# Two pairs of score banks and four banks for the rest, a third unit of 16-wide heads in flight, and first products by sevens in three more layers

## The chip, the cores and the metric

The kernel runs on one core of a Trainium2 chip. The metric is the device time of one execution in microseconds. The core's engines work side by side, each through a queue of its own in the order in which the program was built: PE (TensorE, the matmuls, with its weight loads shown as PEld), DVE (VectorE), ACT (ScalarE), POOL (GpSimd), and SP, which here only issues transfers. Matmuls write to eight accumulator banks (PSUM) of 128 x 512 numbers in 32 bits. A bank is free for a new product when DVE or ACT has read the old one.

## What is computed

A decoder of two layers on an input of 16 sequences of 128 tokens with 256 features, all in 32 bits. Each sublayer is added to the stream and normalized. In order:

```python
x = ln(x + attn0(x))      # 16 heads of 64, causal softmax
x = ln(x + ensemble0(x))  # sum over 8 members: gate_e * proj_out_e . relu(proj_in_e . x), 256 -> 512 -> 256
x = ln(x + experts0(x))   # two shared experts, and 2 of 16 routed experts per token
x = ln(x + attn1(x))      # 16 heads of 16, softmax over a band of +-8 tokens
x = ln(x + cross1(x))     # 16 heads of 16, over a context of 128 tokens
x = ln(x + dense1(x))     # norm_g * sum over 8 experts: w2_e . gelu(w1_e . x + b1_e) + b2_e, 256 -> 512 -> 256
```

## The kernel before

The 16 sequences are four groups (`g` = 0 to 3) of four, 512 tokens each. A sublayer of a group is written as a generator. A planner, `Weaver`, draws from two of them at a time: a main stream of attention and a dense stream (ensembles and experts), by given shares of estimated time, with short follow-ups (norms, transposes, gates, routing) put in ahead of both. A line `yield UNTIL, t` gives a step a due time in the planner's clock. The dense stream's order is ensemble 0, ensemble 1, routed experts for groups 0 and 1, ensemble 2, ensemble 3, routed experts for groups 2 and 3, then the four dense layers of the second decoder layer, 0 to 3. What the planner writes down, the language's scheduler then orders once more for each engine; it gives each tile a buffer from its pool, and the instruction that first writes a reused buffer waits for its last reader.

Products of two sides are cut by a scheme that needs seven block products where eight would do it plainly (`products`): the second product of each ensemble or dense expert always goes so. The stationary blocks (`wb`) are summed once and kept in memory, the sums of the moving blocks (`cm`, L812 to L815) are made by DVE, and the seven partial results are accumulated by DVE (`acc`, L834 and L836). The first product of an expert (256 -> 512, with the hidden result `h`) goes plainly, with eight matmuls of 512 columns per expert, or by sevens with the class `Firsts`, fourteen of 256 columns. Expert 0 of a layer is plain in both cases. By sevens:

- `rows_sums` (DVE, L720) forms sums of the activations once for a layer, in two buffers of the tag `hT`.
- `weight_sums` (POOL, L720 and L746) forms sums of the weights of each expert, in two of the four buffers of the tag `cw`. Routing (`plan`), the gates of the ensembles (`gates0`, `chose`) and the collection of results also use `cw`.
- `steps` runs the seven products in a bank `sums`, held over all four steps, and further banks `other`. ACT copies `sums` to `h` three times (L777, L782, L786) and DVE adds `other` three times (L771). Then `done` applies the relu and the gate (DVE) or Gelu (ACT).

Attention goes by units. In `attention0` a unit is four heads of 64 of one sequence, in `attention16` eight heads of 16 (half the heads of one sequence). A unit passes through score products (`psS`), softmax (`e`: DVE, ACT, and the final scaling on POOL, L380), transposes of the weights (`psO` from `e`, copied by ACT to `eT`, L390), the product with the values, and the output product. In `attention16` POOL first makes masked keys (`kb`, L515). A loop runs over units with fixed distances between these steps, written as `m = n - 2` and the like; `e` has three buffers (tag `p` of the pool `p3`).

The eight banks are shared as follows: score tiles (tag `S`) take two banks each, one such tile in the program; everything else (`bank`, tag `B`: names psH, psM, psO) has six banks.

Of the kernel before, what the change touches and what calls it, by code (L numbers as in the profile page):

```python
# [8 lines left out]
F32 = mybir.dt.float32  # L9
# [5 lines left out]
P = 128  # L15
# [16 lines left out]
def kernel(ctx: ExitStack, tc: tile.TileContext, a: dict, out: bass.AP):  # L32
# [14 lines left out]


    def bank(tag):
        return ps.tile([P, T], F32, tag="B", name=f"ps{tag}", bufs=6)  # L50

    recent = [None]

# [342 lines left out]
    def attention0(x, g):  # L396
        norm = Norm(x)
        norm.bias(bo0)

        def project_quad(g, j):  # L400
            wq, wk, wv, wo = first_quads[j] if g == 0 and j < 2 else load_quad(j)
            xT = xTs[g]
            qT = p2.tile([P, 2, T], F32, tag="qT", name="qT")
            kT = p2.tile([P, 2, T], F32, tag="kT", name="kT")
            for i in range(2):
                c = 2 * j + i
                cols = slice(i * P, (i + 1) * P)
                pq = bank("H")
                project(pq, wq, cols, xT)
                nc.vector.tensor_scalar(  # L410
                    qT[:, i, :], pq, bq0[:, c:c + 1], 0.125, ALU.add, ALU.mult
                )
                pk = bank("H")
                project(pk, wk, cols, xT)
                nc.scalar.activation(kT[:, i, :], pk, AF.Identity, bias=bk0[:, c:c + 1])
                yield 3.44

            v = yield from values(xT, wv, KC)
            heads0[g, j] = qT, kT, v, wo

        def scores(j, b):
            qT, kT, _, _ = heads0[g, j]
            at = slice(b * P, (b + 1) * P)
            s = ps.tile([P, 2, T], F32, tag="S", name="psS", bufs=1)[:, :, :D].rearrange(
                "p s (i k) -> p s i k", i=2
            )

            for i in range(2):
                for k in range(2):
                    rows = slice(64 * k, 64 * k + 64)  # L430
                    with joined(i == k == 0):
                        mm(
                            s[:, k, i, :], lhsT=qT[rows, i, at], rhs=kT[rows, i, at],
                            start=True, stop=True,
                        )
            return softmax(s, causal)

        def output(j, b, zT):
            po = bank("H")[:, :D]
            for i in range(2):  # L440
                mm(po, lhsT=zT[:, i, :], rhs=heads0[g, j][3][:, i, :], start=i == 0, stop=i == 1)
            norm.add(b, po, last=j == 3)

        if (g, 0) not in heads0:
            yield from project_quad(g, 0)
        units = [(j, b) for j in range(4) for b in range(GB)]
        e, eT, zT, at = {}, {}, {}, {}
        for n in range(len(units) + 5):
            if n < 16:
                j, b = units[n]  # L450
                e[n] = scores(j, b)
                at["e", n] = weaver.now + 9.0
                yield 0.6
            m = n - 2
            if m in e:
                yield UNTIL, at["e", m]
                eT[m], _ = weights_T(e.pop(m))
                at["t", m] = weaver.now + 2.5
                yield 0.5
            m = n - 5  # L460
            if m in zT:
                yield UNTIL, at["z", m]
                output(*units[m], zT.pop(m))
                yield 0.86
            m = n - 4
            if m in eT:
                j, b = units[m]
                yield UNTIL, at["t", m]

                pz = bank("O")[:, :D].rearrange("p (c q) -> p c q", c=2)  # L470
                got = eT.pop(m)
                for i in range(2):
                    for k in range(2):
                        h = 2 * i + k
                        with joined(h == 0):
                            mm(
                                pz[64 * k:64 * k + 64, i, :],
                                lhsT=heads0[g, j][2][:, b, 64 * h:64 * h + 64],
                                rhs=got[:, 2 * k + i, :], start=True, stop=True,
                            )  # L480
                zT[m] = p3.tile([P, 2, P], F32, tag="z", name="zT")

                nc.vector.tensor_tensor(  # L483
                    zT[m], pz, bv0[:, 2 * j:2 * j + 2].unsqueeze(2).to_broadcast([P, 2, P]), ALU.add
                )
                at["z", m] = weaver.now + 2.5
                yield 0.6
            if n < 16 and (n < 12 or g + 1 < NG):

                j, b = units[n]  # L490
                if b == 0:
                    ahead = project_quad(g, j + 1) if j < 3 else project_quad(g + 1, 0)
                yield next(ahead)
                if b == 3:
                    assert next(ahead, None) is None
        assert not e and not eT and not zT
        norm.done()


    def attention16(x, qT, kT, v, bv, wo, bo, seen):  # L500
# [9 lines left out]
        def scores(b, c):  # L510

            at = slice(b * P, (b + 1) * P)

            kb = p2.tile([P, 4, P], F32, tag="kb", name="kb")
            nc.gpsimd.tensor_tensor(  # L515
                kb, kT[:, c, at].unsqueeze(1).to_broadcast([P, 4, P]),
                hm4.unsqueeze(2).to_broadcast([P, 4, P]), ALU.mult,
            )
            yield UNTIL, weaver.now + 2.0
            s = ps.tile([P, 2, T], F32, tag="S", name="psS", bufs=1)  # L520
            s = s[:, :, :4 * keys].rearrange("p s (h k) -> p s h k", h=4)
            for k in range(2):
                rows = slice(64 * k, 64 * k + 64)
                for queries, key, _ in parts:
                    mine = slice(b * P + queries.start, b * P + queries.stop)
                    with joined(k == 0 and key == 0):
                        mm(
                            s[queries, k], lhsT=qT[rows, c, mine],
                            rhs=kb[rows, :, key:key + keys], start=True, stop=True,
                        )  # L530
            return softmax(s, seen)
# [37 lines left out]

        units = [(b, c) for b in range(GB) for c in range(2)]  # L570
        e, eT, zT, at = {}, {}, {}, {}
        for n in range(len(units) + 5):
            if n < 8:
                e[n] = yield from scores(*units[n])
                at["e", n] = weaver.now + 12.0
                yield 1.06
            m = n - 2
            if m in e:
                yield UNTIL, at["e", m]
                got = e.pop(m)  # L580
                eT[m] = [weights_T(got[:, 4 * k:4 * k + 4, :]) for k in range(2)]
                at["t", m] = weaver.now + 3.5
                yield 1.0
            m = n - 4
            if ("z", m) in at and units[m][1] == 1:
                yield UNTIL, at["z", m]
                output(units[m][0])
                yield 0.86
            m = n - 3
            if m in eT:  # L590
                yield UNTIL, at["t", m]
                weigh(*units[m], eT.pop(m))
                at["z", m] = weaver.now + 3.0
                yield 0.63
# [337 lines left out]
    def ensemble0(x, xT, g):  # L932
# [13 lines left out]
        def done(to, got, e, i, j):  # L946
# [10 lines left out]
            lambda t: after(  # L957
                products_end(t, norm, None, lambda norm, b: norm.done(b, 2)), tail(1, g)
            ),
            Firsts(xT, done) if g in () else None,  # L960
        )

    def small(tag, n=16, bufs=None):
# [391 lines left out]
    def experts1(x, xT, g, ng):  # L1355
        def load(e):
            return load_up(f"we1_{e}", a["L1_ffn_w1"][e])[0]

        def hidden(h, up, e, c):
            ph = bank("H")  # L1360
            project(ph, up, slice(c * P, (c + 1) * P), xT)
            gelu(h, ph, e, c)

        def gelu(to, one, e, c):
            nc.scalar.activation(to, one, AF.Gelu, bias=b1[:, 4 * e + c:4 * e + c + 1])  # L1365

        def done(to, got, e, i, j):
            for q in range(2):
                gelu(to[:, q], got[:, q], e, 2 * i + q)

        norm = Norm(x)
        for b in range(GB):
            nc.vector.scalar_tensor_tensor(
                out=x[:, b, :], in0=b2sum, scalar=ng[:, b:b + 1], in1=x[:, b, :],
                op0=ALU.mult, op1=ALU.add,
            )
        yield from products(
            load, lambda e: load_blocks(1, e, g, a["L1_ffn_w2"][e]), hidden,
            lambda t: after(products_end(t, norm, ng, lambda norm, b: store(norm, g, b))),
            Firsts(xT, done) if g in (2,3) else None,  # L1380
        )


# [158 lines left out]
```

## Time and profile before

| what | value |
|---|---|
| median of three runs | 1738.57 us (1735.91 to 1738.95) |
| profiled execution, its own time | 1738.27 us |
| span of its trace | 1736.6 us |
| TensorE busy | 1647.3 us, 95% of the span |
| mean granted TensorE clock | 0.975 |
| DVE, ACT, POOL busy | 1164.0, 591.8, 505.5 us |
| stages by time | attention of groups 0 and 1 to about 211 us; ensembles 0 and 1 beside attention of groups 2 and 3 to 545; routing to 615; routed experts to 673; ensembles 2 and 3 beside the second decoder layer's attention to 1040; routed experts to 1144; dense layers after it, alone from 1535 |

The span runs from the first to the last instruction; the execution's own time has 1.7 us around it. Busy time of TensorE includes matmuls that overlap in its pipeline, so the gaps between matmuls, and the granted clock, say more than the share of 95%. In a list of waits a line reads: who waited, for whom, us in total, how many times, the longest. The idle time of an engine that doesn't set the end costs nothing.

### The profile page before, as it was taken

How to read it: one execution, taken by the hardware profiler on the slowest of the kernel's cores; microseconds unless marked ns; L12 is line 12 of the kernel's file. 1: busy time of each engine (PE TensorE's matmuls, PEld its weight loads, DVE VectorE, ACT ScalarE, POOL GpSimd, SP SyncE). 2: the span in 40 equal slices, each digit the busy share in tenths (PEclk: the TensorE clock that was granted, in tenths of full speed). 3: DMA queues.
4: the chain of work that ended last, by engine and by line, in shares of the span. 5: the costliest groups of instructions: out<-in, count | busy, mean ns of one | idle time of the engine just before them, and what ended most of it. 6: DMA issues, size and time to landing. Idle time of an engine off the chain costs nothing.

```text
span 1736.6 us, 22830 instructions
## 1 busy us (share of the span) xinstructions
PE 1647.3 (95%) x8196; PEld 1080.5 (62%) x8196; DVE 1164.0 (67%) x2330; ACT 591.8 (34%) x1360; POOL 505.5 (29%) x543
## 2 busy tenths in 40 slices
PE   9999999999999799999899988998999999999996
PEld 6665656666656465656556655665665665588785
DVE  4565565576677534878796875858769675965655
ACT  4434411111022242103131212643846372654342
POOL 5443532220002302312241315334224132522220
PEclk9999999999998899999999989999999999999998
DMA  9533533432330458422223204671222221124330
GB/s 272 174 118 123 172 140 111 150 112 103 103 110 13 146 186 290 153 93 82 90 79 104 80 31 170 202 245 64 68 91 80 71 70 67 63 83 134 113 121 34
DMA packets 98192, 204.52 MB, mean 118 GB/s; under 512 B 16136, under 2 KB 58176, under 8 KB 98016
## 3 DMA queue, kind: packets, MB, share of 16 engines
q1 hardware_dynamic: 92176, 179.53, 31.2%
q0 software_dynamic: 5904, 23.54, 3.7%
q8 instruction: 65, 1.06, 0.2%
q14 instruction: 47, 0.39, 0.1%
HBM read 172.43 MB, written 37.81 MB: 121 GB/s over the span
## 4 chain that ended last, share of the span: by engine, by line
PE 75%; DVE 12%; DMA 4%; issue 3%; POOL 2%; ACT 1%; SPq 1%; another core or an unknown queue 0%; POOLq 0%; DVEq 0%; ACTq 0%
PE psH L55 40%; PE psM L55 21%; PE psO L60 5%; PE psS L55 4%; PE psO L55 3%; PE psH L60 2%; DVE nmax L358 1%; DVE e L364 1%; DMA wquad<-in_L_attn_W_Q 1%; DMA rows<-copies 1%; DVE total L370 1%; DVE x L311 1%; DVE x L293 1%; DVE acc L836 1%; POOL got L1303 1%
## 5 line engine op out<-in xcount | busy, mean ns | idle before, releaser
L55 PE MATMUL psH<-xT,we 128*128 128x512 f32 (+1 forms) x856 | 397.4, 590 | 0.5 <-DMA we<-in_L_xattn_proj_in 0.5
L380 POOL TENSOR_TENSOR e<-e,inv 128x512 f32<-128x512 f32 (+2 forms) x121 | 159.4, 1319 | 425.6 <-DVE inv L378 369.7
L55 PE MATMUL psM<-cm,wb 128*128 128x256 f32 x1024 | 263.6, 381 | 0.0
L55 PEld LDWEIGHTS psH<-xT,we 128*128 128x128 f32 x856 | 156.8, 191 | 137.0 <-issue 124.9
L55 PEld LDWEIGHTS psM<-cm,wb 128*128 128x128 f32 x1024 | 192.0, 190 | 52.2 <-issue 25.7
L55 PE MATMUL psM<-h,wb 128*128 128x256 f32 x768 | 200.8, 384 | 5.0 <-ACT h L1365 3.4
L836 DVE TENSOR_TENSOR acc<-psM,acc 128x512 f32<-128x512 f32 (+1 forms) x216 | 134.5, 624 | 98.3 <-PE psM L55 98.2
L390 ACT COPY eT<-psO 128x512 f32<-128x512 f32 (+1 forms) x192 | 105.5, 584 | 275.6 <-PE psO L60 261.3
L55 PEld LDWEIGHTS psM<-h,wb 128*128 128x128 f32 x768 | 143.0, 190 | 54.8 <-issue 29.3
L373 ACT ACTIVATE e<-e,nmax 128x128 f32<-128x128 f32 x256 | 99.5, 390 | 139.6 <-DVE nmax L358 113.4
L942 DVE SCALAR_TENSOR_TENSOR h<-psH,gt 128x512 f32<-128x512 f32 x128 | 87.6, 685 | 71.5 <-PE psH L55 71.2
L55 PE MATMUL psH<-xT,wquad 128*128 128x512 f32 x256 | 117.2, 601 | 6.1 <-DMA wquad<-in_L_attn_W_Q 5.4
L515 POOL TENSOR_TENSOR kb<-kT,hm 128x512 f32<-128x512 f32 x64 | 72.4, 1134 | 159.1 <-PE psS L55 104.5
L60 PEld LDWEIGHTS psO<-ident,e 128*128 128x128 f32 (+1 forms) x768 | 85.2, 133 | 48.2 <-issue 35.9
L60 PE MATMUL psO<-ident,e 128*128 128x128 f32 (+1 forms) x768 | 109.7, 280 | 2.0 <-POOL e L380 2.0
L1365 ACT ACTIVATE h<-psH,b 128x512 f32<-128x512 f32 (+1 forms) x100 | 60.6, 623 | 104.7 <-PE psH L55 95.9
L369 ACT ACTIVATE e<-e 128x576 f32<-128x576 f32 (+1 forms) x64 | 55.7, 871 | 88.2 <-DVE e L364 87.9
L55 PEld LDWEIGHTS psH<-xT,wquad 128*128 128x128 f32 x256 | 46.7, 190 | 58.9 <-issue 47.8
L309 POOL TENSOR_TENSOR rstd<-ve,mhalf 128x4 f32<-128x4 f32 (+1 forms) x32 | 28.9, 903 | 177.9 <-DVE ve L307 177.6
L370 DVE TENSOR_REDUCE total<-e 128x8 f32<-128x576 f32 (+1 forms) x64 | 62.8, 981 | 24.6 <-ACT e L369 24.0
L55 PE MATMUL psO<-eT,v 128*64 128x128 f32 (+2 forms) x1024 | 76.6, 313 | 0.0
L55 PE MATMUL psH<-wquad,zT 128*128 128x256 f32 x256 | 67.8, 388 | 4.8 <-DVE zT L483 2.5
(240 smaller groups left out, 2624.0 us busy)
## 6 DMA issues: line engine op xcount, KB each, us to landing
wb<-wbd SPq DMA_DIRECT2D x56, 896.0 KB
we<-in_L_xattn_proj_in SPq DMA_DIRECT2D x32, 512.0 KB
wt<-table SPq DMA_DIRECT2D x64, 256.0 KB
we<-in_L_ffn_w SPq DMA_DIRECT2D x32, 512.0 KB
wbd<-wb POOLq DMA_DIRECT2D x16, 896.0 KB
gt<-gatesd SPq DMA_DIRECT2D x32, 256.0 KB
results<-y SPq DMA_DIRECT2D x10, 768.0 KB
rows<-copies SPq DMA_DIRECT2D x6, 1024.0 KB
```

The source lines that it names most:

```text
L55: recent[0] = nc.tensor.matmul(*args, **how)
L60: return nc.tensor.transpose(out_, in_, ident[:n, :n])
L309: nc.gpsimd.tensor_tensor(rstd[:, at], ve[:, at], mhalf[:, at], ALU.pow)
L369: nc.scalar.activation(e, e, AF.Exp)
L370: nc.vector.tensor_reduce(total, e, AX.X, ALU.add)
L373: nc.scalar.activation(e[:, h, :], s[:, h // (n // 2), h % (n // 2), :], AF.Exp, bias=nmax[:, h:h + 1], accum_out=total[:, h:h + 1],)
L380: engine.tensor_tensor(e, e, inv.unsqueeze(2).to_broadcast([P, n, keys]), ALU.mult)
L390: return eT, nc.scalar.copy(eT, pt)
L515: nc.gpsimd.tensor_tensor(kb, kT[:, c, at].unsqueeze(1).to_broadcast([P, 4, P]), hm4.unsqueeze(2).to_broadcast([P, 4, P]), ALU.mult,)
L836: nc.vector.tensor_tensor(to, pm[:, :len(slots), :], to, ALU.add)
L942: nc.vector.scalar_tensor_tensor(out=h, in0=ph, scalar=0.0, in1=gates[e], op0=ALU.max, op1=ALU.mult)
L1365: nc.scalar.activation(to, one, AF.Gelu, bias=b1[:, 4 * e + c:4 * e + c + 1])
```

## The change

Three edits.

1. The banks: the tag `B` goes from six banks to four, the tag `S` from one tile of two banks to two tiles. Eight banks are in use as before.
2. In `attention16` the distances of the steps grow by one: transposes of a unit come three scores later, the product with the values four, the output five.
3. `Firsts` is used for the first products of the ensembles of groups 0 and 1, and of the dense layer of group 1; before, only the dense layers of groups 2 and 3 had it.

```diff
     def bank(tag):
-        return ps.tile([P, T], F32, tag="B", name=f"ps{tag}", bufs=6)
+        return ps.tile([P, T], F32, tag="B", name=f"ps{tag}", bufs=4)
...
         def scores(j, b):
...
-            s = ps.tile([P, 2, T], F32, tag="S", name="psS", bufs=1)[:, :, :D].rearrange(
+            s = ps.tile([P, 2, T], F32, tag="S", name="psS", bufs=2)[:, :, :D].rearrange(
...
             yield UNTIL, weaver.now + 2.0
-            s = ps.tile([P, 2, T], F32, tag="S", name="psS", bufs=1)
+            s = ps.tile([P, 2, T], F32, tag="S", name="psS", bufs=2)
...
-        for n in range(len(units) + 5):
+        for n in range(len(units) + 6):
             if n < 8:
                 e[n] = yield from scores(*units[n])
                 at["e", n] = weaver.now + 12.0
                 yield 1.06
-            m = n - 2
+            m = n - 3
             if m in e:
...
-            m = n - 4
+            m = n - 5
             if ("z", m) in at and units[m][1] == 1:
...
-            m = n - 3
+            m = n - 4
             if m in eT:
...
-            Firsts(xT, done) if g in () else None,
+            Firsts(xT, done) if g in (0,1) else None,
...
-            Firsts(xT, done) if g in (2,3) else None,
+            Firsts(xT, done) if g in (1,2,3) else None,
```

## The prediction

> **What bounds the kernel now.** I read four views. First the page: busy time per engine and the clock row.
>
> ```profile
> span 1736.6 us, 22830 instructions
> ...
> PE   1647.3 (95%) x8196; PEld 1080.5 (62%) x8196; DVE 1164.0 (67%) x2330; ACT 591.8 (34%) x1360; POOL 505.5 (29%) x543
> ```
>
> TensorE is the bound as a whole: 89 us of the span are without it, no other engine is above 67%. The table by stage (columns: length, then busy us of PE, weight loads, DVE, ACT, POOL, then granted clock, DMA share, GB/s) tells where those 89 us lie.
>
> ```profile
> 50.00:100.00 50.00, 47.38 (x289) 30.96 (x288) 27.23 (x54) 22.65 (x82) 21.93 (x27) 1.00 0.41 141
> 211.00:545.00 334.00, 332.29 (x1418) 209.41 (x1418) 211.91 (x411) 54.65 (x192) 68.38 (x95) 1.00 0.33 114
> 545.00:615.00 70.00, 56.30 (x294) 37.23 (x293) 41.84 (x117) 22.50 (x86) 18.49 (x19) 0.85 0.27 91
> 615.00:673.00 58.00, 52.90 (x319) 38.41 (x317) 20.21 (x59) 26.14 (x74) 0.00 (x0) 0.94 0.72 245
> 1040.00:1144.00 104.00, 92.61 (x537) 60.90 (x536) 67.70 (x133) 47.22 (x111) 41.64 (x33) 0.95 0.57 186
> 1144.00:1535.00 391.00, 376.93 (x1877) 230.93 (x1877) 287.90 (x535) 205.46 (x280) 135.87 (x113) 0.99 0.25 85
> 1535.00:1720.00 185.00, 182.48 (x840) 156.35 (x839) 114.61 (x215) 74.97 (x155) 42.99 (x55) 1.00 0.33 107
> ```
>
> Where an ensemble or a dense layer runs (211 to 545, and from 1535), TensorE idles 1.7 us in 334 and 2.5 in 185: a product removed there is time removed. The idle time sits around routing (545 to 615) and the routed experts (615 to 673, 1040 to 1144), which the edits don't shorten. The list of waits, TensorE's own, shows what the score banks cost; the timeline shows one such gap (in brackets: idle time before, and its releaser).
>
> ```profile
> PE psS L55 <- DVE e L352: 7.7, 7, 2.2
> PE psS L55 <- DVE e L364: 3.9, 4, 1.8
> PE psO L60 <- POOL e L380: 2.0, 2, 1.1
> 57.83 0.71 PE L55 MATMUL psS<-kT,qT 64*128 64x128 f32 x8 [0.86 <-DVE e L352]
> ```
>
> Last the chain in order of time, four plain first products of 512 columns, and then one expert of a layer that already has first products by sevens (a matmul is two records, so x16 is eight):
>
> ```profile
> 930.11 3.43 PE psH L55 x8
> ...
> 1659.90 3.45 PE psM L55 x16
> 1663.36 0.86 PE psH L55 x4
> 1664.22 0.86 PE psM L55 x4
> 1665.09 0.86 PE psH L55 x4
> 1665.95 2.59 PE psM L55 x12
> 1668.54 0.86 PE psH L55 x4
> 1669.40 1.73 PE psM L55 x8
> 1671.13 0.86 PE psH L55 x4
> 1671.99 3.45 PE psM L55 x16
> ```
>
> The expert takes 12.09 us, back to back, for 28 products of 256 columns: 0.432 us each.
>
> **The change part by part.** The sum is made against the profiled execution, 1738.27 us (span 1736.6 and 1.7 around it); the median of the runs is 1738.57, so 0.3 is added at the end. It counts on the order in which the two programs issue their instructions, which the changed kernel's build gives (no time is in it).
>
> *First products by sevens, ensembles g=0 and 1, dense layer g=1.* Per expert 1 to 7, eight products of 512 columns go and fourteen of 256 come. Four of 512 take 3.43 us (the first line of the fence), so eight take 6.86; fourteen at 0.432 take 6.05. That is 0.81 us by 7 experts by 3 layers: **-17.0 us**, all on the bound engine, in stages without gaps.
> What comes with it lies beside TensorE. DVE: three additions per expert of 0.688 us (row L771) and four subtractions of 0.418 per layer: 63 x 0.688 + 12 x 0.418 = 48 us; the ensembles' four relu-and-gate steps per expert stay four of 512 elements (0.685). ACT: three copies of 0.586 per expert, 37 us; in the dense layer eight Gelu of 256 (0.50 and 0.46) for four of 512 (0.688), 8 us more; six table loads of 1.283 fewer by the built order, 8 us less. POOL: three of 0.73 and one of 0.81 per expert, 63 us. The totals become DVE 1212, ACT 629, POOL 568 of some 1720 us: 70, 37 and 33%, still cover. If DVE's cover were gone, its 48 us would be the price. No DMA is added; the weight loads keep their three buffers.
> The additions wait for ACT's copy and for TensorE. In DVE's queue they stand ahead of the accumulations and the gating, which TensorE's next banks wait for. POOL's weight sums wait for a load or for a `cw` buffer, which the gate layer also uses (its eight `chose` tiles fall into ensemble g=1); behind them in POOL's queue stand the softmax scaling (L380) and the key masks (L515). In the built order the scaling has at least 5.6 us of TensorE work as cover beyond the first 190 us of that work, as before (5.1). I take **+1 us** for all of this: the only layers with sevens in the trace lose 0.83 and 0.28 us to the copy L782 and nothing to POOL. Ends: 0 and +12 (half a microsecond at each of 21 experts, and 1.5 at the shared buffers).
>
> *Second pair of score banks, third unit.* The waits of the fence and one of 0.2 sum to 13.8 us. In the built order the waits of score matmuls for DVE fall from 89 to 31. The five 0.86 us gaps of the first layer had no TensorE work between a score and the next; now they have 0.43, so 0.43 us each is left (2.2). The rest have 1.7 or more. So at most -11.6. A gap removed from a queue in order is partly met again at the next wait, so I take half: **-6 us** (ends 0 and -11.6).
> The third unit has its limits. The tile `e` has three buffers (p3), so the softmax of unit n, which writes `e` on DVE (L352, or L364 after its maximum), must wait for the transposes of unit n-3. The built order shows four units scored and three in softmax at most steps, before three and two: the unit is real. Behind that waiting DVE step stand the accumulations of the dense layer.
>
> *Four banks for the rest.* The trace of before has no bank shortage, so I bound it. The cover of a wait is the TensorE work between the last matmul that the releaser depends on and the matmul that waits. Waits with under 1.5 us of cover go from 61 to 169: in the routed experts from 21 to 102, elsewhere from 40 to 67.
> What a release costs, by rows: DVE starts 0.03 us after TensorE ends, and a bank of 512 takes 0.69:
>
> ```profile
> 1638.16 1.03 PE L55 MATMUL psM<-tx,we 128*128 128x256 f32 x4
> 1639.22 0.69 DVE L771 TENSOR_TENSOR h<-psM,h 128x512 f32<-128x512 f32 x1 [0.17 <-PE psM L55]
> ```
>
> So 0.8 us of cover is enough if the reader's queue is empty; one step ahead of it costs up to 0.69. In the routed experts the new bank wait is for the copy L1242, 0.266 us against 0.43 of cover: free, unless the tanh (0.28), a copy (0.37) or an exponential (1.06) stands ahead on ACT. There are 34 waits under 0.7 us there (before: 1). At 0.3 us that is 10; I take 5, since the first such stage is held by its loads (DMA busy at 1.0 of its 16 engines from 640 to 660). Elsewhere 27 more, with DVE busy two thirds of the time, at a quarter of a microsecond: 7. Together **+12 us**; ends 0 and 108 x 0.35 = 38.
>
> A rule that speaks against the change: the Trainium skill, "TensorE: Matmul & The Clock Gate", section "A second HAM failure mode: psum-queue depth-cycling", says that cycling through accumulator banks leaves TensorE micro-idle so often that its clock falls back and forth. The row comes first: from 50 to 100 it idles 2.6 us in short gaps and the clock stays 1.00. With the row the 12 us cost 12. By the rule the two expert stages (58 and 104 us, at 0.94 and 0.95) could fall to the 0.85 of 545 to 615, some 16 us more, 1745. I take the row, and keep the 16 for the upper end.
>
> Sum: 1738.27 - 17.0 + 1 - 6 + 12 = 1728.3; with 0.3, **1728 us**.
>
> **The rivals.**
> 1. *Bank shortage outweighs the products (slower).* Place: the 108 new short covers, in the expert stages and where DVE is over 70% busy (287.9 of 391 us from 1144 to 1535). With a reader's step ahead at every second one, 0.35 us each: 1738.3 - 17 + 1 - 6 + 38 = 1754. It makes the kernel slower by more than the bound from 0.24 us per short cover on. For it: banks fall by a third. Against: covers of 0.43 to 0.85 left gaps of 0.2 to 0.5 us before, or none, outside the chains of norms and routing.
> 2. *A late POOL or DVE takes the gain (no change).* The weight sums hold up the softmax scaling or DVE meets its buffer waits for `e`: +11 beside the sum, 1739. For: the trace has POOL waiting up to 8 us for TensorE at L720. Against: the cover of L380 above.
> 3. *The second score pair and the third unit do nothing*, because the gaps move to the next wait: 1734.6.
> 4. *Banks cost next to nothing*, as the 40 short covers elsewhere do before, and the score waits go: 1738.3 - 17 + 1 - 11 + 3 = 1714.
>
> **How the numbers follow.** Forecast 0.42 (own range 1721 to 1735), rival 4 0.18, rival 3 0.12, rival 2 0.10, rival 1 0.18. A measurement of this kernel tells about 0.2% from no change, 3.5 us: faster is below 1735.1, slower above 1742. Rival 3 lies on that edge and is split. Faster 0.68, same 0.14, slower 0.18. The range goes from rival 4 to the middle of rival 1 (with part of the clock's 16 us): 1713 to 1748.
>
> **What would show it.** Right: TensorE's busy time down by some 17 us; the stage of the two ensembles shorter by about 11 us and still with hardly a gap; waits of psS for DVE from 11.6 us to about 2 to 5; new waits of TensorE for ACT (L1242, L1257, L390) and DVE in the expert stages, 5 to 10 us; clock there as before. Wrong: waits of psH, psM or psO for DVE or ACT of over 25 us in total (rival 1), or for POOL L720 or L380 of over 5 (rival 2); or a clock under 0.9 in the expert stages.

## The result, and the profile after

The change makes the kernel slower: 1750.64 us (median of six runs, 1744.91 to 1753.72) against 1738.80 for the kernel before (six runs, 1735.91 to 1742.33), a ratio of 1.0064 with a 95% interval of 1.0046 to 1.0082. That is some 11 us more, where I forecast 10 less. The profiled execution is the fastest of the six (1744.91 us, span 1743.2), so its trace shows 6.6 us of the difference to the profiled execution before, not the whole. Part of the rest is TensorE's granted clock: 0.979 in this execution, 0.974 to 0.977 in the other five (0.003 of 1743 us is some 5 us, an estimate).

First the page of the changed kernel, span and busy time per engine.

```profile
span 1743.2 us, 23681 instructions
...
PE 1636.8 (94%) x8448; PEld 1126.1 (65%) x8448; DVE 1209.6 (69%) x2406; ACT 626.0 (36%) x1445; POOL 577.3 (33%) x626
```

The work is as forecast: DVE 1209.6 (1212 was said), ACT 626.0 (629), POOL 577.3 (568). The columns that TensorE is given, at the 3.43 us for four products of 512, fall by 18 us. Its busy time fell by only 10.5 (1647.3 to 1636.8), not by the 17 that I had named as a sign, and the time without TensorE grew from 89 us (1736.6 - 1647.3) to 106 (1743.2 - 1636.8). The table by stage of the changed kernel (length, busy us of PE, weight loads, DVE, ACT, POOL, granted clock, DMA share, GB/s), with the stages of the prediction's table from the ensembles to the end of attention, shows where.

```profile
207.00:529.00 322.00, 321.58 (x1569) 239.96 (x1570) 240.08 (x454) 76.20 (x225) 112.67 (x147) 1.00 0.35 117
529.00:599.00 70.00, 55.29 (x306) 37.34 (x305) 43.39 (x121) 24.16 (x95) 18.56 (x19) 0.90 0.26 91
599.00:658.00 59.00, 53.47 (x317) 38.72 (x317) 19.77 (x58) 25.88 (x72) 0.00 (x0) 0.94 0.71 239
1030.00:1138.00 108.00, 96.92 (x536) 63.49 (x534) 68.03 (x137) 48.51 (x110) 41.36 (x33) 0.94 0.55 179
1138.00:1545.00 407.00, 376.80 (x1975) 247.10 (x1974) 306.24 (x564) 217.65 (x327) 161.79 (x142) 0.99 0.24 83
```

The ensembles (first row) keep the promise: hardly a gap, and between the first product of an ensemble and the first of routing 336.9 us pass (206.9 to 543.8) instead of 348.6 (211.7 to 560.3), 11.7 us less. In all runs of this document the same stretch is 335.9 to 340.2 us with these sevens and 348.1 to 350.4 without. The loss is in the fifth row, in which the second layer's attention of groups 2 and 3 runs beside the dense layers of groups 0 and 1. Before, it had 376.93 us of TensorE in 391; now it has 376.80 in 407, so its idle time went from 14 to 30 us. DVE is busy 75% of that stage, as before (74%).

From the list of TensorE's waits in the changed kernel (who waited, for whom, us in total, times, longest):

```profile
PE psH L55 <- DVE r_one L1011: 8.4, 2, 4.8
PE psH L55 <- DVE zT L483: 8.0, 5, 6.3
...
PE psS L55 <- POOL kb L515: 3.4, 1, 3.4
...
PE psO L55 <- DVE acc L836: 3.2, 2, 2.1
...
PE psO L60 <- ACT eT L390: 3.0, 2, 2.4
PE psM L55 <- DVE acc L836: 2.8, 2, 2.6
...
PE psM L55 <- ACT eT L390: 2.4, 5, 1.0
...
PE psS L55 <- DVE e L352: 2.0, 5, 0.4
```

The waits of score products for DVE are gone but for 2.0 us (11.6 before). In their place stand waits of the other names, psO and psM, for the readers of their banks: the accumulation L836, the copy of the transposes L390. No line names one culprit; each is a few us. So I sum them in two classes: all waits of psH, psM and psO for DVE or ACT, and all waits of psS. The first went from 37.7 to 70.4 us, the second from 15.2 to 5.4 (with one wait of 3.4 us for POOL's masked keys in each; before, the list calls it "issue").

These sums mix two things. A product can wait for a bank, or for its own operand: the first two lines of the fence, `r_one` and `zT`, are operands that come out of the chains of norms and routing. The single gaps of the timeline tell them apart: a gap is counted to a bank when its releaser read a bank and did not write an operand of the product. Counted so, the waits of psH, psM and psO for a bank went from 1.1 to 29.9 us, those of psS from 11.7 to 2.0.

One expert with first products by sevens is as fast as before: 12.08 us from the start of its first block of second products to that of the next expert (1666.54 to 1678.62), 12.09 before.

### The profile page after: what moved, and what is told of

The parts are those of the page before. It is cut to its first block, busy times and chain, and to the rows that moved or that the text cites. A ratio compares the mean times of both kernels' runs of the same rounds, so it can differ in the third digit from the quotient of the medians.

```text
span 1743.2 us, 23681 instructions
## 1 busy us (share of the span) xinstructions
PE 1636.8 (94%) x8448; PEld 1126.1 (65%) x8448; DVE 1209.6 (69%) x2406; ACT 626.0 (36%) x1445; POOL 577.3 (33%) x626
## 4 chain that ended last, share of the span: by engine, by line
PE 67%; DVE 18%; issue 5%; ACT 4%; DMA 3%; POOL 3%; SPq 1%; another core or an unknown queue 0%; POOLq 0%; DVEq 0%; ACTq 0%
PE psH L55 33%; PE psM L55 23%; PE psO L60 4%; PE psO L55 3%; PE psS L55 2%; DVE nmax L358 2%; DVE e L364 2%; DVE total L370 2%; PE psH L60 2%; DVE acc L836 1%; DMA rows<-copies 1%; ACT e L369 1%; DVE h L942 1%; POOL copies L1127 1%; DMA wquad<-in_L_attn_W_Q 1%
## 5 line engine op out<-in xcount | busy, mean ns | idle before, releaser
L380 POOL TENSOR_TENSOR e<-e,inv 128x512 f32<-128x512 f32 (+2 forms) x120 | 162.0, 1351 | 317.5 <-DVE inv L378 251.0
L55 PE MATMUL psH<-xT,we 128*128 128x512 f32 (+1 forms) x604 | 257.6, 553 | 7.3 <-DVE x L293 3.8
L55 PE MATMUL psM<-h,wb 128*128 128x256 f32 x768 | 201.6, 385 | 12.1 <-DMA wb<-wbd 3.0
L836 DVE TENSOR_TENSOR acc<-psM,acc 128x512 f32<-128x512 f32 (+1 forms) x216 | 134.9, 625 | 92.8 <-PE psM L55 92.4
L55 PEld LDWEIGHTS psM<-h,wb 128*128 128x128 f32 x768 | 141.7, 190 | 57.3 <-issue 20.1
L55 PEld LDWEIGHTS psH<-xT,we 128*128 128x128 f32 x604 | 111.0, 191 | 96.1 <-issue 72.7
L390 ACT COPY eT<-psO 128x512 f32<-128x512 f32 (+1 forms) x192 | 106.2, 582 | 161.4 <-PE psO L60 145.7
L515 POOL TENSOR_TENSOR kb<-kT,hm 128x512 f32<-128x512 f32 x64 | 72.7, 1140 | 126.3 <-PE psS L55 71.1
L720 POOL TENSOR_TENSOR sw<-we 128x256 f32<-128x256 f32 x70 | 56.4, 806 | 168.4 <-PE psM L55 131.1
L771 DVE TENSOR_TENSOR h<-psM,h 128x512 f32<-128x512 f32 x105 | 72.2, 688 | 43.3 <-PE psM L55 41.1
L309 POOL TENSOR_TENSOR rstd<-ve,mhalf 128x4 f32<-128x4 f32 (+1 forms) x32 | 28.9, 902 | 172.8 <-DVE ve L307 172.7
L55 PEld LDWEIGHTS psH<-xT,wquad 128*128 128x128 f32 x256 | 46.7, 190 | 55.4 <-issue 48.5
L1365 ACT ACTIVATE h<-h,b 128x256 f32<-128x256 f32 x126 | 57.2, 500 | 70.1 <-DVE h L771 70.0
```

What stands on the lines that cost most here:

```text
L55: recent[0] = nc.tensor.matmul(*args, **how)
L380: engine.tensor_tensor(e, e, inv.unsqueeze(2).to_broadcast([P, n, keys]), ALU.mult)
L390: return eT, nc.scalar.copy(eT, pt)
L515: nc.gpsimd.tensor_tensor(kb, kT[:, c, at].unsqueeze(1).to_broadcast([P, 4, P]), hm4.unsqueeze(2).to_broadcast([P, 4, P]), ALU.mult,)
L720: engine.tensor_tensor(to, one, two, ALU.subtract)
L771: nc.vector.tensor_tensor(block(i, j), other, block(i, j), ALU.add)
```

## The experiments

Four sets of runs, each beside runs of the kernel before on the same chip. Before took 1738.80 us on the chip of the first comparison, and 1727.8 to 1730.1 on those of the experiments, so ratios are compared and not times (0.1% is 1.7 us). In the traces that difference between chips lies in the routing of the first layer: from its first product to the shared experts 17.7 us are lost to TensorE before and 16.4 after on the first chip, 4.7 to 7.5 in every run of the others. It says nothing of the change. The kernel before has a trace on the first chip alone, so the row of before below stands for another chip than the rows from e6 on.

For each run the table gives the ratio, the two sums of TensorE's waits, and the time lost in two stages. The lost time is a stage's length less its columns at 3.43 us for four products of 512, so it holds gaps and any lower clock alike. "For a bank" are the waits of psH, psM and psO that are no waits for an operand, as told above; "psS, bank" is the same for the score tiles. "Experts" is the second stage of routed experts, "last" the stage of the fifth row above, ended by the last product of `gw`. The waits and lost times come from one profiled execution each.

| kernel | ratio to before (95%) | waits psH, psM, psO for DVE, ACT | of these for a bank | waits psS | psS, bank | lost, experts | lost, last |
|---|---|---|---|---|---|---|---|
| before (first chip) | 1 | 37.7 | 1.1 | 15.2 | 11.7 | 11.2 | 14.3 |
| after (first chip) | 1.0064 (1.0046 to 1.0082) | 70.4 | 29.9 | 5.4 | 2.0 | 15.3 | 33.8 |
| e6: the change again | 1.0045 (1.0027 to 1.0063) | 64.7 | 28.5 | 5.4 | 2.0 | 15.2 | 31.2 |
| e1: sevens only | 0.9909 (0.9890 to 0.9928) | 36.7 | 4.1 | 14.9 | 14.8 | 6.4 | 20.4 |
| e2: banks only (4, two score tiles) | 1.0070 (1.0053 to 1.0087) | 54.7 | 21.0 | 5.4 | 2.0 | 16.7 | 27.6 |
| f2: four banks, one score tile | 1.0128 (1.0108 to 1.0148) | 53.2 | 23.6 | 11.9 | 7.2 | 15.7 | 31.2 |
| f3: five banks, one score tile | 1.0019 (1.0008 to 1.0031) | 40.6 | 5.6 | 14.1 | 10.5 | 12.1 | 17.8 |
| e3: third unit only | 1.0033 (1.0018 to 1.0048) | 36.5 | 1.2 | 20.1 | 10.7 | 14.1 | 14.3 |
| e4: banks and sevens | 0.9967 (0.9951 to 0.9983) | 48.5 | 24.5 | 4.4 | 4.4 | 10.4 | 23.2 |
| e5: banks and third unit | 1.0069 (1.0052 to 1.0087) | 45.2 | 16.4 | 12.8 | 5.6 | 17.9 | 17.9 |
| e8: third unit and sevens | 0.9995 (0.9984 to 1.0006) | 39.5 | 2.0 | 21.8 | 17.1 | 13.3 | 26.3 |
| e7: the change, dense layer 1 plain | 1.0025 (1.0012 to 1.0039) | 53.9 | 18.4 | 5.4 | 2.0 | 15.1 | 24.3 |

Differences in us are ratios times 1728. A ratio is good to 2 to 3.5 us, the difference of two runs to 4 or 5.

### Each edit alone

Sevens only: the two lines with `Firsts`.

```diff
-            Firsts(xT, done) if g in () else None,
+            Firsts(xT, done) if g in (0,1) else None,
...
-            Firsts(xT, done) if g in (2,3) else None,
+            Firsts(xT, done) if g in (1,2,3) else None,
```

> Only the first products by sevens in the three layers; six banks, one score tile and the old distances stay. If the bank shortage took the gain (rival 1), this one is faster than before by what the products save, 12 to 17 us: 1722 to 1727. If the added work of DVE, ACT and POOL took it (rival 2), it is near or above before: 1736 to 1750, with the loss in the last stage of attention beside dense layer 1.

Measured: 1713.78 us beside 1728.46, 0.9909, -15.7 us. The forecast for this part was -17.0 + 1 = -16. This kernel is faster than before and after.

Banks only:

```diff
-        return ps.tile([P, T], F32, tag="B", name=f"ps{tag}", bufs=6)
+        return ps.tile([P, T], F32, tag="B", name=f"ps{tag}", bufs=4)
...
-            s = ps.tile([P, 2, T], F32, tag="S", name="psS", bufs=1)
+            s = ps.tile([P, 2, T], F32, tag="S", name="psS", bufs=2)
```

(The same for the scores of `attention0`.)

> Only the banks: two score tiles, four banks for the rest. Bank shortage: 1752 to 1770, above before by what the change lost (some 29 us) less the score gaps. Added work of the sevens: 1733 to 1740, since no such work is there.

Measured: 1741.57 us, 1.0070, +12.1 us. The gain of the second score tile is in this figure already, so the four banks alone must cost more than the 12 that I gave them. TensorE's waits for a bank, both classes together, went from 12.8 to 23.0 us: 10 of the 12.

Third unit only:

```diff
-        for n in range(len(units) + 5):
+        for n in range(len(units) + 6):
...
-            m = n - 2
+            m = n - 3
...
-            m = n - 4
+            m = n - 5
...
-            m = n - 3
+            m = n - 4
```

> Only the third unit in flight, with six banks and one score tile. If the three buffers of e or the longer distances cost DVE time (a third theory), it is 5 to 15 us slower than before: 1744 to 1754. By the other two theories it is within 3 us of before.

Measured: 1733.45 us, 1.0033, +5.7 us: a loss, where I had counted a share of a gain. The waits of psS went up, from 15.2 to 20.1, but not those for a score tile (11.7 and 10.7): 4.7 us of the rise are two waits for DVE's routing.

The change without the third unit (the first two diffs together):

> The change without its third unit. By the bank theory it is as slow as the change, 1748 to 1755. If the third unit is the culprit, it is at the forecast of 1728. If the parts need each other (third unit hides short banks), it is slower than the change, 1755 to 1770.

Measured: 1723.25 us, 0.9967, -5.7 us. The sum of e1 and e2 is -3.6, so these two edits hardly meet. With the third unit the same kernel is the change, at 1.0045 and 1.0064. Adding the third unit turns a gain into a loss.

### The banks taken apart; the other pairs

The change without sevens, and the change once more:

> The change without the sevens. The single effects were: banks +12 us, third unit +6. If they add, this is 18 us above before. If four banks and the third unit hurt each other (a unit more holds banks and softmax tiles while only four banks turn over), it is 24 us or more above, since the whole change was 9 us slower than the sum of its parts.

> The change itself once more, on the chip of the other three. Its ratio to before was 1.0064 on another chip; 1.004 to 1.009 is expected. If it is at 1.001 (the sum of the parts measured apart), the missing interaction is only a difference between chips.

Measured: 1.0069 and 1.0045. Had banks and third unit added up, e5 would be 18 us above before; it is 12. Beside e2 (1.0070), with the new banks and plain first products in the three layers, the third unit costs nothing; on the old banks (e3) it cost 5.7 us. And the sevens, worth 15.7 us alone, bring 4 in the whole change: the two intervals even overlap.

Four banks with one score tile (two banks idle), and five with one score tile (one idle):

```diff
-        return ps.tile([P, T], F32, tag="B", name=f"ps{tag}", bufs=6)
+        return ps.tile([P, T], F32, tag="B", name=f"ps{tag}", bufs=4)
```

(`bufs=5` in the second.)

> Four banks for the rest and one score tile: two banks lie idle. It parts the cost of the shortage from the gain of the second score tile. If the second score tile gains the 6 us forecast, this is 18 us above before (banks alone: 12). If it gains nothing, or costs, because scores taken early hold up softmax tiles, this is at +12 or below.

> Five banks for the rest, one score tile, one bank idle. If shortage grows steeply as banks go, this is within 3 us of before; if each bank is worth the same, half of what four banks cost.

Measured: 1749.01 and 1730.54 us beside 1727.84, 1.0128 and 1.0019. Going from six banks to five costs 3 us, from five to four another 19. From f2 to e2 the second score tile takes 0.58% back, 10 us, close to the ceiling of 11.6 that I had read from the waits. The lost time of the last stage follows: 14.3, 17.8, 31.2. So do the waits for a bank, both classes together: 12.8, 16.1 and 30.8 us. That is 3.3 and 18 us more than before, where the times are 3.3 and 22 longer. The list of waits of f2, last stage only, shows where a bank came late:

```profile
PE psM L55 <- ACT h L1365: 3.4, 5, 0.8
PE psM L55 <- DVE acc L836: 2.6, 1, 2.6
...
PE psM L55 <- ACT eT L390: 1.8, 1, 1.8
```

The second and third are products of the dense layers that wait for a bank's reader. The first is so in two of its five gaps; in the other three the product takes `h` as its operand. One wait for a bank lasts 2.6 us, more than the reader's own step (0.69 for 512 columns): just ahead of that reader, in the timeline, stands a sum (L815) of 2.36 us for a median of 0.68, beside a POOL step (L284).

### The third unit and the sevens together

The change with dense layer 1 plain (`g in (2,3)` kept in the second `Firsts` line), and third unit with sevens on the old banks:

> The change, but dense layer 1 keeps its plain first products: sevens only in the two ensembles. If the loss is made in the last stage with attention, where dense layer 1 by sevens, the third unit and four banks meet (the stages' tables put some 14 us of extra idle time there), this is 10 us or more faster than the change although it has 6 us more TensorE work: 1.000 of before or below. If the ensembles' own sevens meet the shortage, it stays at 1.006 or above.

> The change with the old banks (six and one score tile): third unit and sevens. If only banks make the two hurt each other, the single effects add: -15.7 + 5.7, ratio 0.994. If the third unit and the sevens collide on DVE, whatever the banks, it is at before or above it: 1.000 to 1.006.

Measured: 1.0025 and 0.9995. Without the sevens in dense layer 1 the change is no slower than with them: in that layer they bring nothing under the other two edits. It isn't 10 us faster either, so that layer alone doesn't make the loss. And the third unit costs 14.9 us beside sevens (0.9909 to 0.9995) even with six banks, so it isn't four banks that make it dear. Nor is it waits for banks: both classes together are 18.9 us in e1 and 19.1 in e8, and from e4 to e6, with the third unit on the new banks, they go from 28.9 to 30.5 while the time grows by 13.5. The sums by name mislead here. Of the rise of psS from 14.9 to 21.8, 3.4 us are one wait for POOL's masked keys; of the rise of the other names from 48.5 to 64.7 (e4, e6) only 4 are for banks.

Part of it is the clock. The time that a lower granted clock takes ((1 - clock) times the span, mean over the executions) is 35.1 us in e1 and 40.6 in e8, beside 37.3 and 38.4 in the runs of before on the same chips: some 4 of the 14.9 us, an estimate. The trace of e8 shows the granted clock at 0.50 behind a gap. The same score products take 2.08 us there and 1.13 a little later:

```profile
1053.14 2.08 PE L55 MATMUL psS<-kb,qT 64*128 64x512 f32 x4 [3.37 <-POOL kb L515]
...
1059.66 1.13 PE L55 MATMUL psS<-kb,qT 64*128 64x512 f32 x4
```

TensorE's gaps as a whole grow by 5.9 us between the two traces (1714.6 - 1626.5 and 1727.0 - 1633.0), which are 12.4 us apart.

A candidate for the cause was the three buffers of `e`. In the changed kernel DVE idles 14.8 us at L352 for the transposes of the unit three before (4.0 before). Four buffers for `e` need room, so first the tile `v` was cut to two buffers, then `e` got four:

```diff
-        v = p3.tile([P, GB, D], F32, tag="v", name="v")
+        v = p3.tile([P, GB, D], F32, tag="v", name="v", bufs=2)
...
-        e = p3.tile([P, n, keys], F32, tag="p", name="e")
+        e = p3.tile([P, n, keys], F32, tag="p", name="e", bufs=4)
```

(The first edit alone in the first kernel; `late`, of the same tag as `v`, goes with it.)

> A control for the next: the change with the values' tile v in two buffers instead of three (memory is needed for the next). It may cost some us by itself: 1.004 to 1.012.

> As g1, with four buffers for the softmax tile e instead of three. If the third unit costs because its softmax waits on DVE for a tile e (DVE idle at L352 for the transposes: 4.0 us before, 14.8 after), this is 5 to 15 us faster than g1. If the banks are what is short, it is within 3 us of g1.

DVE's own waits, first with three buffers of `e`, then with four:

```profile
DVE e L352 <- PE psO L60: 14.2, 15, 1.6
```

```profile
DVE e L352 <- PE psO L60: 2.4, 5, 0.9
```

The wait is gone; the time is 1.0046 (1.0028 to 1.0063) and 1.0034 (1.0023 to 1.0045). The difference is 0.1%, give or take 0.2%, so of the 13.5 us at most some 5 lie there. The buffers of `e` are not the main cause.

Last, the sevens on the old banks (e1), with the third unit in one of the two attentions, or for two of the four groups:

```diff
+        far = 3 if seen is not None else 2
-        for n in range(len(units) + 5):
+        for n in range(len(units) + 3 + far):
...
-            m = n - 2
+            m = n - far
...
-            m = n - 4
+            m = n - far - 2
...
-            m = n - 3
+            m = n - far - 1
```

This is the banded attention; the others have `seen is None` (attention over the context), `g < 2`, and `g >= 2`; `g` is passed down for the last two.

> Sevens with six banks (e1, ratio 0.991), and the third unit in the banded attention alone. Both parts together make 0.9995. If the cost lies in the larger tiles of cross attention (DVE steps of 1.2 us), this stays at 0.991 to 0.993; if in the banded one, 0.997 to 1.000; if each carries half, 0.995.

> As h1, with the third unit in cross attention alone: 0.997 to 1.000 if the larger tiles carry the cost, 0.991 to 0.993 if the banded attention does, 0.995 if both.

> Sevens with six banks, and the third unit for groups 0 and 1 alone (beside ensembles 2 and 3 and the second routed experts). If its cost is in the stage of routed experts (7 us more idle time there in the stage table), 0.995 to 0.997; if all of it is in the last stage, 0.991.

> Sevens with six banks, and the third unit for groups 2 and 3 alone (beside dense layers 0 and 1). If the last stage carries half of the cost, 0.994 to 0.996; if DVE's load by the sevens in dense layer 1 carries all, 0.998 to 1.000.

| third unit, beside sevens, in | ratio (95%) | above e1 (0.9909) | lost, experts | lost, last |
|---|---|---|---|---|
| nowhere (e1) | 0.9909 (0.9890 to 0.9928) | | 6.4 | 20.4 |
| the banded attention (h1) | 1.0000 (0.9986 to 1.0014) | +0.0091 | 15.5 | 30.6 |
| the attention over the context (h2) | 0.9945 (0.9926 to 0.9963) | +0.0036 | 16.3 | 19.4 |
| groups 0 and 1 (h3) | 0.9981 (0.9970 to 0.9993) | +0.0072 | 13.3 | 24.4 |
| groups 2 and 3 (h4) | 0.9949 (0.9932 to 0.9967) | +0.0040 | 6.2 | 24.0 |
| everywhere (e8) | 0.9995 (0.9984 to 1.0006) | +0.0086 | 13.3 | 26.3 |

The banded attention alone carries a loss as large as the whole, and more than the other (0.91 against 0.36%). The parts add up to more than the whole by both divisions, but the difference isn't clear of the intervals, and h3 came out above both of its forecasts.

The places don't agree with where the units run. Groups 2 and 3 (h4) leave the stage of routed experts alone (6.2) and add in the last one; but groups 0 and 1 (h3) add 4.0 in the last stage too, in which no unit of theirs runs. And h1 loses 9.1 us more beside the routed experts, although no banded unit is scored there: its banded scores (64 x 288) stop at 980 us and start again at 1171, and the stage lies between 1034 and 1117. What changes in that stage is a few single gaps. TensorE waits 3.4 us for POOL's masked keys and 4.1 for DVE's `hh`, the hidden result of the routed experts, in e8, 3.3 and 4.1 in h3; in e1 and h4 not at all and 0.8 and 0.7. The kernel before has these gaps too (3.4 and 4.0). So a third unit in one place also moves other work: the planner draws its order anew for each kernel. That this order, and not the load of a queue, makes part of the loss is a rival that no run here tests.

## Why the prediction was wrong, point by point

Two steps of it failed. The four banks were priced at 12 us and cost 22, because the price counted a bank's reader and at most one step ahead of it. And the third unit had no price of its own and cost 13.5. The second score tile brought 4 us more than I took, which doesn't make up for it.

My sum was 1738.27 - 17.0 + 1 - 6 + 12. Term by term, in us:

| term | forecast | measured | from |
|---|---|---|---|
| sevens, with their load on DVE, ACT, POOL | -16 | -15.7 | e1 |
| four banks for the rest | +12 | +22 | f2 |
| second score tile | -6, together with the third unit | -10 | f2 to e2 |
| third unit | in the -6 | +13.5 with sevens and banks | e4 to e6 |
| sum | -10 | +10 | the change: +11, and +8 in e6 |

The last two terms are differences along a chain of runs that ends at the change itself, so that the sum comes near it is no test of them.

*Sevens.* Right in size and in their own cover. The ensemble stage became 11.7 us shorter (11 was said), the fewer columns were a full gain there, and no wait of TensorE for L720 or L380 is in the list. That -15.7 is so near to -16 is partly luck: e1 lost 4.8 us less than before beside the routed experts and 6.1 more in the last stage, and neither was in my sum. Right as well was the granted clock of the change. The expert stages had 0.94 and 0.95 and have 0.94 and 0.94, and on one chip the median of the whole is 0.980 for e6 and 0.979 for the kernel before, though waits of psH, psM and psO for a bank went from 1.1 to 28.5 us. The rule on cycling accumulator banks in the Trainium skill, "TensorE: Matmul & The Clock Gate", section "A second HAM failure mode: psum-queue depth-cycling", of which I had made a fall to 0.85 and some 16 us, did not show in them.

*Four banks.* The step that failed is "So 0.8 us of cover is enough if the reader's queue is empty; one step ahead of it costs up to 0.69", with the line drawn at 1.5 us. In the built order the last stage had 2 waits with less than that before, and four banks make it 8 (e2): by my price 2 us. Measured are 27.6 us lost instead of 14.3. The stage has DVE at three quarters busy with softmax steps of 1.2 us, so a bank's reader can have several steps ahead of it, as below. With the line at 3 us the counts read 21 before, 40 with five banks, 95 with four (one score tile), and the lost time 14.3, 17.8, 31.2. That line is set after the result, to three kernels; it wasn't tested on another. I had put 5 of my 12 us on the routed experts, with the copy L1242 as the releaser. That copy is not in TensorE's waits of the changed kernel or of f2 at all, and in the second stage of routed experts f2 lost 4.5 us more than before (15.7, 11.2), against 17 in the last stage.

The timeline of the changed kernel shows one such queue (start, duration, engine, line; in brackets the idle time before and its releaser).

```profile
1311.76 1.90 POOL L380 TENSOR_TENSOR e<-e,inv 128x1024 f32<-128x1024 f32 x1 [2.75 <-DVE inv L378]
1312.09 2.12 DVE L813 TENSOR_TENSOR cm<-h 128x512 f32<-128x512 f32 x1
1314.13 1.21 DVE L358 TENSOR_REDUCE nmax<-psS 128x8 f32<-128x1024 f32 x1
...
1321.45 1.23 DVE L836 TENSOR_TENSOR acc<-psM,acc 128x512 f32<-128x512 f32 x2
1322.14 0.64 PE L55 MATMUL psO<-eT,v 128*32 128x256 f32 x8 [2.05 <-DVE acc L836]
```

A sum of DVE (L813) that usually takes 0.69 us takes 2.12 beside POOL's scaling. Then come a maximum, the rest of the sums, and three more steps of 1.2 us (L370, L364, L370), hardly with a pause. The accumulation L836 starts some 10 us after the POOL step began and over 2 us after the products that it adds, and the product psO, which needs the bank that L836 reads, waits 2.05 us. The long sum is at most 1.4 us of this (2.12 - 0.69); the queue of steps is the rest.

*Second score tile.* I took half of the ceiling of 11.6, since "a gap removed from a queue in order is partly met again at the next wait". It brought 10 us, nearly all of it, give or take 5. The ceiling itself was not read cleanly: the 13.8 us that I summed hold 2.0 of transposes that wait for POOL's scaling (L380), which is no wait for a score tile; without them the ceiling is 9.6.

*Third unit.* The failed step is the heading itself, "second pair of score banks, third unit", for which I gave one gain. I wrote that the unit is real and that `e` limits it, and gave it no price of its own. Alone it cost 5.7 us, with the banks and plain products nothing, with sevens 13.5 to 14.9. That last pairing no term of mine could have shown, since each edit was costed against the kernel before. The sevens put additions (L771), copies and Gelus of the dense layer into the same queues, and one bank (`sums`) is held over four steps; that these are what makes the third unit dear is my reading. It fits e5 and e8, but it wasn't isolated, and the planner's new order is its rival. What is shown: the loss needs no four banks (e8), little of it is a shortage of `e` buffers (g2), it is larger in the banded attention (h1, h2), some 4 us of it come with a lower clock (e1, e8, an estimate), and almost none of it is a wait for a bank. What makes up the rest stays open.

*The rivals.* Rival 1 named the right sign: 1754 was its time. The sign that I had given for it, waits of psH, psM or psO for DVE or ACT "of over 25 us in total", was useless as written, since the kernel before has 37.7 already; as growth it came, with 70.4 - 37.7 = 32.7. Of its two places, the stage with DVE over 70% busy was right and the expert stages were minor. And banks alone do not decide: e4 has the four banks and is faster than before. Rival 2's late POOL did not come: in the list POOL's masked keys (`kb`, L515) hold TensorE once, for 3.4 us, as before the change, and L720 and L380 not at all. Its DVE half, waits at the buffers of `e`, came and cost little (g2). Rivals 3 and 4 fall with f2.

## What to carry to other kernels

Cost a loss of accumulator banks by the queue of the bank's reader in the stage where it is busiest, not by the reader's own step; with DVE at 75% the counts here follow a line of 3 us of cover better than one of 1.5 (a fit to three kernels), and the price was steep (3 us for the first bank, 19 for the second). Give each part of a compound edit a term with a sign of its own, also the one that "only" deepens a pipeline, and run the pairs: the sevens alone are worth 15.7 us (the best version run, 0.9909), and all but 4 of it went when they were combined with four banks and a third unit. When no single line of TensorE's waits stands out, sum them by class of bank, and leave out the waits for a product's own operand: only then did the sums tell that the banks' cost is waits for banks and the third unit's is not.

## What the runs showed of the hardware

A DVE step with both inputs in SBUF can be held up by a POOL step: L813 took 2.12 us beside an L380 of 1.90 us that had begun 0.33 us earlier, and ended 0.55 us after it, against a median of 0.69. That agrees with the Trainium skill, "SBUF — State Buffer", section "Who interferes with whom", by which the two share one read path when DVE has two SBUF inputs. The price over the run is visible: the 256 sums L812 to L815 lie 18.5 us above their medians in the kernel before and 23.2 in the one after, and each of those that took over 0.1 us too long (31 and 36) overlaps a POOL step. I had not counted it. The change added only 4.7 us of it, beside 28.8 us of new waits for banks, so by itself it isn't the main cause of the result. But a long sum stands ahead of the late reader in both waits for a bank looked at above, in the changed kernel and in f2; what fewer banks would cost without such sums, no run shows.

TensorE's clock is granted at half speed in short stretches, of which some stand behind gaps: in e8 it is 0.50 from 1053.3 to 1056.3, behind a gap of 3.37 us, and the products there take 2.08 us for 1.13. A gap can so cost more than its own length.
